# Norm, transposes and routing of a mixture's tokens by pairs of tiles inside the attention before it, and its results added and normed by pairs inside the attention after it

## Chip, cores, metric

The kernel runs on one core of one Trainium2 chip. The metric is the device time of one execution in microseconds (us); the median of five runs of the kernel before is 2369.61. The engines are PE (matrix multiply, with its weight loads shown apart as PEld), DVE (vector), ACT (scalar, activation tables), POOL (GpSimd) and SP, which only issues transfers.

## What is computed

Four layers in sequence, each an attention and a feed-forward part with a layer norm after each. x has 1024 tokens of 256 values in fp32. The change lies between the first attention, the first mixture of experts and the second attention. From the reference:

```python
# layer 0, attention: windowed, two softmaxes per head, 16 heads
    out = jnp.einsum('bhqk,bhkd->bhqd', diff, v)
    return out.transpose(0, 2, 1, 3).reshape(B, S, H * hd) @ Wo
...
# layer 0, mixture: 8 experts, each token goes to 2 of them
    router_logits = jnp.einsum('bsh,he->bse', hidden_states, Wr)
    topk_logits, selected = jax.lax.top_k(router_logits, TOP_K)
    router_probs = jax.nn.softmax(topk_logits, axis=-1)
    for e in range(NUM_EXPERTS):
        w_e = jnp.where(selected == e, router_probs, 0.0).sum(axis=-1, keepdims=True)
        g = jnp.clip(jax.nn.silu(jnp.einsum('bsh,hi->bsi', hidden_states, Wg[e])), -7.0, 7.0)
        u = jnp.einsum('bsh,hi->bsi', hidden_states, Wu[e])
        out = out + jnp.einsum('bsi,ih->bsh', g * u, Wd[e]) * w_e
...
# layer 1, attention: causal, 16 heads of 128
    q = (x @ Wq + bq).reshape(b, h, t, dh)
    k = (x @ Wk + bk).reshape(b, t, h, dh).transpose(0, 2, 3, 1)
    v = (x @ Wv + bv).reshape(b, t, h, dh).transpose(0, 2, 1, 3)
...
def _layernorm(x, axis=-1, eps=1e-05):
    return (x - m) / jnp.sqrt(v + eps)
```

After each part, x = layernorm(x + part). In layer 1 the queries are reshaped without a transpose. So the four heads of one group of queries come from 256 consecutive rows of x, while its keys and values come from all rows.

## The kernel before

x stays on the chip as `k.x`, eight tiles of 128 tokens by 256, and beside it its transpose `k.xT`, which the projections read. `transpose_two(t)` (L163) turns two tiles with four PE transposes into one bank of PSUM and copies them to `xT` on DVE (L178). `norm_half` (L191) norms four tiles: `bn_stats` and `bn_aggr` for each (L202, L203), one square root on ACT (L221) and a reciprocal on DVE (L222), then one DVE step for each tile (L206). `power` (L211) gives the same factor without ACT: one step on DVE, then a power on POOL (L215).

The stages run one after another (L1954 on): at the start of most, four calls of `transpose_two`; at the end of attn0, ffn0 and attn1, `layernorm`. Each stage takes its own buffers, laid over those of the stage before. Inside the loops marked `in_order` (L140) the instructions of PE, ACT, DVE and POOL keep the order in which the program writes them. Instructions outside such a loop, and SP's transfers, are put among them by a planner. In the trace, for instance, the statistics of tiles 0 to 3 after attn0 run at 271 us, before attn0's loop has ended.

**attn0** (L438). 32 units, four groups g of heads by eight tiles t. Unit i makes scores for its tile (L591 and L601 on PE, maximum L609 on DVE, eight exponentials L617 on ACT), then a difference of two softmaxes (L625 to L645 on DVE, ACT and POOL). Three units later `attn0_values` transposes it (L654, copied to pt on ACT at L656), multiplies by the values (L660, copied to ot on ACT at L666), projects (L672), and DVE adds the result to x (L227). So in iteration i tile t of unit i - 3 is finished, tile 0 of the last group at i = 27 and tile 7 at i = 34. The last projections of operands (`operands`, L508), which read `xT`, are through by i = 28. After i = 31 no new unit starts: three iterations only drain.

**ffn0** (L689). It stores x to DRAM as `moe_rows` in two halves (L706) and loads the weights of all experts as `gu` and `wd` with 24 transfers of 256 KB (L712, L715). The router's logits come from 16 matmuls (L739), and each tile's two experts from `max` and `max_index` (L744, L745). From L748 on the tokens are sorted by expert into 23 blocks of 128, up to `tokens` (L824). POOL then gathers each block's rows from `moe_rows` by an indirect transfer (L853, issued at L845); two matmul steps per block, and SP stores the result to `moe_results` (L894). After the loop, for each tile and each of its two experts, a gather (L916) and a DVE step that adds it, weighted, to x (L917). Then `layernorm`.

**attn1** (L931). Weights `wq` (four), `wk`, `wv`, `wo` from a pool of ten buffers. `make_queries(g, j)` (L963) projects 256 columns of `xT` and DVE adds the bias and scales (L969), writing every sixteenth element; 16 of them make group g. `make_keys` (L974) is evicted by ACT (L979), `make_values` by DVE (L988). `pieces` (L993) lists these in order. Before the first scores (L275) `ensure` runs all 16 queries of group 0 and one piece of keys; the others go between the units of the loop at L1048.

Of the kernel before, what the change touches and what calls it, by code (L numbers as in the profile page):

```python
# [25 lines left out]
I32 = mybir.dt.int32  # L26
U32 = mybir.dt.uint32
AF = mybir.ActivationFunctionType
ALU = mybir.AluOpType
AX = mybir.AxisListType  # L30

P = 128
# [10 lines left out]
class Kit:  # L43
# [147 lines left out]
    def norm_half(self, half):  # L191
        tiles = range(4 * half, 4 * half + 4)
        stats = self.tile("st", [P, 4, 2])
        for t in tiles:
            self.add_stats(t, stats)
        rstd = self.rsqrt(stats[:, :, 1], 4, LN_EPS)
        for t in tiles:
            self.norm_tile(t, stats, rstd)

# [5 lines left out]
    def norm_tile(self, t, stats, rstd):  # L205
        self.nc.vector.tensor_scalar(  # L206
            self.x[:, t, :], self.x[:, t, :], stats[:, t % 4, 0:1], rstd[:, t % 4 : t % 4 + 1],
            ALU.subtract, ALU.mult,
        )
# [8 lines left out]
    def rsqrt(self, v, n, eps, scale=1.0, tag=None):  # L218
# [3 lines left out]
        self.nc.vector.reciprocal(r, r)  # L222
        return r

    def add_rows(self, t, y):
# [212 lines left out]
def attn0(k, a):  # L438
# [92 lines left out]
    def make_values(t):  # L531
# [11 lines left out]
        even.append(vt)  # L543

    runs = [(g, half) for g in range(4) for half in range(2)]
    with k.in_order():
        for _ in operands(*runs[0]):
# [3 lines left out]
        for i in range(len(units) + 3):  # L551
# [25 lines left out]
            if i - 1 in made:  # L577
                made[i - 1] = next(made[i - 1])
            for _ in ending:
                pass  # L580

# [107 lines left out]
def ffn0(k, a):  # L689
# [8 lines left out]
    wd = k.tile("wd", [P, 8, NC, D])  # L698
    rows = k.tile("dram", [T, D], tag="moe_rows")
    results = k.tile("dram", [blocks * P, D], tag="moe_results")  # L700
    wr = k.weights([P, NC, 8], a["L0_ffn_Wr"].rearrange("(c p) e -> p c e", p=P))
    ternary_tiles = list(ffn1_weights(k, a))
    for tile_ in ternary_tiles[:2]:
        next(tile_)
    for half in range(2):
        nc.sync.dma_start(  # L706
            out=rows[half * HALF : (half + 1) * HALF, :].rearrange("(t p) d -> p t d", p=P),
            in_=k.x[:, 4 * half : 4 * half + 4, :],
        )
    for e in range(8):  # L710
# [24 lines left out]


    ps = k.bank()[:, : NT * 8].rearrange("p (t e) -> p t e", t=NT)
    for t in range(NT):
        k.project_rows(ps[:, t, :], lambda c: wr[:, c, :], t * P)  # L739
    logits, top = small([P, NT, 8]), small([P, NT, 8])  # L740
    which = small([P, NT, 8], U32)
    nc.vector.tensor_copy(logits, ps)
    for t in range(NT):
        nc.vector.max(top[:, t, :], logits[:, t, :])  # L744
        nc.vector.max_index(which[:, t, :], top[:, t, :], logits[:, t, :])  # L745
    chosen, mine = small([P, 2, NT]), k.tile("route", [P, 2, NT, 8], tag="mine", bufs=1)
# [43 lines left out]
    nc.vector.tensor_reduce(slot, mine.rearrange("p k t e -> p (k t) e"), axis=AX.X, op=ALU.add)  # L790
    slots = k.tile("route", [P, 2 * NT], I32, tag="slots", bufs=1)
    nc.vector.tensor_copy(slots, slot)
# [42 lines left out]

    prob = k.tile("route", [P, 2, NT], tag="prob", bufs=1)
    p1, p2 = prob[:, 0, :], prob[:, 1, :]
# [5 lines left out]

    def gather(out, source, index):
        nc.gpsimd.indirect_dma_start(  # L845
            out=out, out_offset=None, in_=source,
            in_offset=bass.IndirectOffsetOnAxis(ap=index, axis=0),
        )

    taken_rows, xTs, hs, hTs = {}, {}, {}, {}  # L850
    for b in range(blocks):
        taken_rows[b] = k.tile("rows", [P, D])
        gather(taken_rows[b], rows, tokens[:, b : b + 1])  # L853

# [41 lines left out]
    with k.in_order():  # L896
        turned(0)
        for b in range(blocks + 2):
# [10 lines left out]
            if 0 <= tile_ < len(ternary_tiles):  # L909
                next(ternary_tiles[tile_], None)  # L910
                if not late and tile_ + 2 < len(ternary_tiles):
                    next(ternary_tiles[tile_ + 2])
    for t in range(NT):
        for i in range(2):
            y = k.tile("rows", [P, D])
            gather(y, results, slots[:, i * NT + t : i * NT + t + 1])  # L916
            nc.vector.scalar_tensor_tensor(  # L917
                k.x[:, t, :], y, prob[:, i, t : t + 1], k.x[:, t, :], ALU.mult, ALU.add
            )

# [10 lines left out]
def attn1(k, a):  # L931
# [5 lines left out]
    nc.sync.dma_start(out=bq, in_=a["L1_attn_bq"])  # L937
    nc.sync.dma_start(out=bk, in_=a["L1_attn_bk"])
    wq, ws, queries, keys, values = [], {}, {}, {}, {}

# [22 lines left out]
    def make_queries(g, j):  # L963
        if j == 0:
# [3 lines left out]

        nc.vector.tensor_scalar(  # L969
            queries[g].rearrange("p h (t j) -> p h t j", j=16)[:, :, :, j],  # L970
            ps.rearrange("p (h t) -> p h t", h=4), bq[:, j : j + 1], scale, ALU.add, ALU.mult,
        )

# [55 lines left out]
    def attend(g, h, half, pts):  # L1029
# [12 lines left out]
        if h == 3:  # L1042
            yield from add_up(g, half)

    beside = ffn2_weights(k, a)
    with k.in_order():
        pipe = Pipe(k)
        for count, (g, h, half, s) in enumerate(units):  # L1048
# [142 lines left out]
def attn2(k, a):  # L1191
# [249 lines left out]
    def finish(ch, half, out, outs):  # L1441
# [34 lines left out]
        for s in range(4):  # L1476
            k.norm_tile(4 * half + s, stats, rstd)
            if s % 2:
                yield
# [470 lines left out]
def four_layers(ctx: ExitStack, tc: tile.TileContext, a, out):  # L1950
# [3 lines left out]
    for stage in STAGES:  # L1954
        with k.scope(**SCOPES[stage]):

            for t in {ffn1: (), ffn2: (), attn2: (0, 2)}.get(stage, range(0, NT, 2)):
                k.transpose_two(t)
            stage(k, a)
            if stage in (attn0, ffn0, attn1, attn3):  # L1960
                k.layernorm()
# [76 lines left out]
```

## Time and profile before

| | us |
|---|---|
| median of five runs (2367.59 to 2369.75) | 2369.61 |
| the profiled execution | 2364.6 |
| its span, first to last instruction | 2362.9 |
| PE busy in the span | 2168.4 (92%) |
| DVE, ACT, POOL busy | 1225.2, 893.1, 489.5 |
| last add to x in attn0 (L227), start | 291.86 |
| first gather of rows (L845), start | 314.53 |
| first gather of results (L845), start | 404.42 |
| last DVE step that adds a result (L917), start | 426.37 |
| first scores of attn1 (L275), start | 450.50 |
| granted clock of PE over the span | 0.969 |

The profile follows one execution. Its times are from the span's start. A granted clock of 1 is PE at full speed. A share of DMA is the mean busy share of the core's 16 DMA engines. The duration shown for several matmuls on one line is from the start of the first to the end of the last. The profiled execution is 5.0 us faster than the median of the runs that were timed by themselves.

### The profile page before, as it was taken

The numbers are of one execution on the slowest core, as the hardware profiler recorded it, in microseconds if no ns is written. First come the engines' busy times: TensorE is split into PE (matmuls) and PEld (weight loads), VectorE is DVE, ScalarE is ACT, GpSimd is POOL, SyncE is SP. The second block draws the span as 40 slices with busy tenths as digits, with TensorE's granted clock in tenths as the row PEclk, the third lists the DMA queues.
The fourth block names the chain that finished last, engine by engine and source line by source line (L and its number), as shares of the span: only waits on it lengthen the run. The fifth ranks groups of instructions, "written<-read, shape, count | busy, mean of one in ns | idle before, by whom it ended". The sixth has DMA issues, their size and how long they took to land.

```text
span 2362.9 us, 25437 instructions
## 1 busy us (share of the span) xinstructions
PE 2168.4 (92%) x8595; PEld 1227.1 (52%) x8595; DVE 1225.2 (52%) x2734; ACT 893.1 (38%) x2328; POOL 489.5 (21%) x630
## 2 busy tenths in 40 slices
PE   8999777799999999998988998899999997999997
PEld 4666544466656655664444443455555564444443
DVE  5677556565665646555763445544544554222223
ACT  3666524134343434344453222454544451111111
POOL 4333122222232323321110000332222220000000
PEclk9999979899999999999999999999999998999999
DMA  5100153011101101013100010000000000111000
GB/s 168 35 19 20 62 185 109 23 41 36 50 23 60 57 27 41 18 54 126 47 2 10 28 53 27 2 1 19 1 18 10 10 1 18 36 45 45 20 1 18
DMA packets 59218, 92.24 MB, mean 39 GB/s; under 512 B 8944, under 2 KB 33584, under 8 KB 59088
## 3 DMA queue, kind: packets, MB, share of 16 engines
q1 hardware_dynamic: 54176, 78.15, 10.3%
q0 software_dynamic: 4912, 12.46, 1.9%
q8 instruction: 69, 1.13, 0.2%
q14 instruction: 61, 0.50, 0.1%
HBM read 69.76 MB, written 17.17 MB: 37 GB/s over the span
## 4 chain that ended last, share of the span: by engine, by line
PE 78%; DVE 11%; ACT 6%; issue 2%; POOL 1%; DMA 1%; SPq 0%; DVEq 0%; ACTq 0%; POOLq 0%
PE bank L152 23%; PE wide L275 10%; PE wide L297 7%; PE bank L1034 5%; PE bank L262 5%; PE bank L1811 5%; PE bank L159 4%; ACT e L617 3%; PE bank L683 3%; PE bank L1019 2%; PE bank L1402 1%; PE bank L1150 1%; PE bank L869 1%; DVE st L609 1%; PE bank L672 1%
## 5 line engine op out<-in xcount | busy, mean ns | idle before, releaser
L152 PE MATMUL bank<-xT,w 128*128 128x512 f32 (+2 forms) x1520 | 660.4, 564 | 2.0 <-DVE xT L178 1.7
L152 PEld LDWEIGHTS bank<-xT,w 128*128 128x128 f32 (+1 forms) x1520 | 286.2, 193 | 279.6 <-issue 259.6
L253 POOL TENSOR_SCALAR p<-p,st 128x128 f32<-128x128 f32 (+7 forms) x256 | 191.0, 746 | 682.2 <-DVE st L252 537.7
L275 PE MATMUL wide<-k,q 128*128 128x512 f32 (+3 forms) x768 | 290.4, 487 | 3.6 <-ACT p L245 2.7
L266 ACT COPY pt<-bank 128x512 f32<-128x512 f32 (+3 forms) x384 | 170.9, 480 | 307.8 <-PE bank L262 304.6
L275 PEld LDWEIGHTS wide<-k,q 128*128 128x128 f32 x768 | 142.5, 190 | 140.5 <-issue 124.8
L240 DVE TENSOR_REDUCE st<-wide 128x1 f32<-128x128 f32 (+7 forms) x256 | 194.0, 758 | 14.7 <-POOL p L253 0.5
L297 PE MATMUL wide<-t,w 128*128 128x512 f32 (+1 forms) x392 | 187.5, 600 | 3.9 <-DVE t L1679 2.4
L262 PE MATMUL bank<-ident,p 128*128 128x128 f32 x1152 | 169.1, 274 | 18.9 <-POOL p L253 18.9
L262 PEld LDWEIGHTS bank<-ident,p 128*128 128x128 f32 x1152 | 137.9, 141 | 83.2 <-issue 38.8
L1929 DVE TENSOR_TENSOR t<-t,bank 128x512 f32<-128x512 f32 (+1 forms) x66 | 45.4, 688 | 257.4 <-PE bank L152 257.4
L1928 ACT ACTIVATE t<-bank 128x512 f32<-128x512 f32 (+1 forms) x66 | 39.4, 597 | 324.5 <-PE bank L152 319.7
L1034 PE MATMUL bank<-pt,v 128*128 128x512 f32 (+3 forms) x384 | 139.3, 487 | 0.0
L235 DVE TENSOR_TENSOR wide<-wide,causal 128x128 f32<-128x128 f32 x256 | 74.7, 292 | 122.2 <-PE wide L275 121.1
L1811 PE MATMUL bank<-pt,v 128*128 128x512 f32 x288 | 137.2, 596 | 0.0
L245 ACT ACTIVATE p<-wide,st,factor 128x128 f32<-128x128 f32 (+7 forms) x128 | 106.4, 831 | 71.3 <-DVE st L242 70.6
L297 PEld LDWEIGHTS wide<-t,w 128*128 128x128 f32 (+1 forms) x392 | 67.9, 189 | 109.4 <-issue 47.4
L159 PE MATMUL bank<-w,xT 128*128 128x512 f32 (+3 forms) x320 | 123.5, 523 | 0.0
L245 ACT ACTIVATE p<-wide,st 128x128 f32<-128x128 f32 (+7 forms) x128 | 95.0, 742 | 65.1 <-DVE st L240 64.5
L617 ACT ACTIVATE e<-wide,st 128x128 f32<-128x128 f32 x256 | 89.8, 377 | 49.9 <-DVE st L609 34.7
L1427 ACT ACTIVATE pt<-wide 128x1024 f32<-128x1024 f32 (+3 forms) x96 | 75.4, 810 | 69.1 <-PE wide L1421 67.6
L227 DVE TENSOR_TENSOR x<-bank,x 128x256 f32<-128x256 f32 x120 | 49.8, 421 | 87.3 <-PE bank L1019 34.5
(302 smaller groups left out, 3042.6 us busy)
## 6 DMA issues: line engine op xcount, KB each, us to landing
w<-in_L_ffn_gate_up_dram SPq DMA_DIRECT2D x16, 512.0 KB
w<-in_L_attn_Wq_dram SPq DMA_DIRECT2D x12, 512.0 KB
w<-in_L_attn_Wo_dram SPq DMA_DIRECT2D x12, 512.0 KB
rows<-parts SPq DMA_DIRECT2D x16, 256.0 KB
w<-in_L_ffn_down_dram SPq DMA_DIRECT2D x8, 512.0 KB
w<-in_L_attn_Wk_dram SPq DMA_DIRECT2D x7, 512.0 KB
w<-in_L_attn_Wv_dram SPq DMA_DIRECT2D x6, 512.0 KB
moe_results<-y SPq DMA_DIRECT2D x23, 128.0 KB
```

The costliest lines, as they stand in the source:

```text
L152: self.nc.tensor.matmul(out, lhsT=weight(c), rhs=self.xcols(c, lo, n), start=c == 0, stop=c == NC - 1)
L159: self.nc.tensor.matmul(out, lhsT=self.xcols(c, lo, n), rhs=weight(c), start=c == 0, stop=c == NC - 1)
L240: nc.vector.tensor_reduce(top, scores[:, :n], axis=AX.X, op=ALU.max, negate=True)
L245: nc.scalar.activation(probs[:, :n], scores[:, :n], AF.Exp, bias=top, scale=1.0 if scale is None else scale, accum_out=total,)
L253: self.nc.gpsimd.tensor_scalar(probs[:, :n], probs[:, :n], total, 1.0, ALU.mult, ALU.mult)
L262: self.nc.tensor.transpose(ps[:, i * P : (i + 1) * P], probs[:, (lo + i) * P : (lo + i + 1) * P], self.ident,)
L266: self.nc.scalar.copy(pts[lo // 4][:, :n, slot * P : (slot + 1) * P], ps[:, : n * P].rearrange("p (b q) -> p b q", b=n),)
L275: self.nc.tensor.matmul(s[:, lo : lo + m], lhsT=query, rhs=key(lo, m), start=True, stop=True)
L297: nc.tensor.matmul(acc[m][:, half * HALF : (half + 1) * HALF], lhsT=down[:, m * P : (m + 1) * P], rhs=h, start=i == 0, stop=i == count - 1,)
L617: nc.scalar.activation(e[:, r, f, b, :], sc[:, r, f, b, :], AF.Exp, bias=top[:, at : at + 1], accum_out=total[:, at : at + 1],)
L1034: nc.tensor.matmul(out[:, lo:], lhsT=values[g, b][:, h * P : (h + 1) * P], rhs=pts[b // 4][:, b % 4, lo:], start=b == 0, stop=b == 4 * hal ...
L1811: nc.tensor.matmul(out, lhsT=values[i][:, g * P : (g + 1) * P], rhs=pts[i // 4][:, i % 4, :], start=i == 0, stop=i == b,)
```

## The change

At the end of attn0 a generator `close(t)` takes tiles t and t + 1, for t = 0, 2, 4, 6, in four steps, one per iteration: statistics of tile t; statistics of tile t + 1 and the factor (`power`, but `rsqrt` for the last pair); norm of both tiles, a store of both to `moe_rows`, and `transpose_two`; routing of both with their `max` and `max_index`. The first step follows in the iteration in which tile t is finished. The router's weights `wr` are loaded at attn0's start into a buffer of their own, and ffn0 no longer norms, transposes, stores `moe_rows` or routes.

At the end of ffn0 the gathers of results, the adding and the norm are gone. In attn1 all 16 gathers are issued first, into eight buffers of the pool `ot`. Then `close(t)` adds, norms and transposes two tiles, and after each up to six pieces of the queries of group 0 are projected. The evictions of these 16 pieces move from DVE to ACT, with the bias scaled beforehand. The transposes at attn1's start go.

```diff
+    def close(t, last=False):
+        stats = k.tile("st", [P, 4, 2], tag="stats", bufs=2)
+        k.add_stats(t, stats)
+        yield
+        k.add_stats(t + 1, stats)
+        at = t % 4
+        rstd = (k.rsqrt if last else k.power)(stats[:, at : at + 2, 1], 2, LN_EPS)
+        yield
+        for i in range(2):
+            k.norm_tile(t + i, stats, rstd[:, i : i + 1])
+        nc.sync.dma_start(
+            out=k.rows[t * P : (t + 2) * P, :].rearrange("(t p) d -> p t d", p=P),
+            in_=k.x[:, t : t + 2, :],
+        )
+        k.transpose_two(t)
+        yield
+        ps = k.bank()[:, :16].rearrange("p (t e) -> p t e", t=2)
+        for i in range(2):
+            k.project_rows(ps[:, i, :], lambda c: wr[:, c, :], (t + i) * P)
+        nc.vector.tensor_copy(logits[:, t : t + 2, :], ps)
+        for i in (t, t + 1):
+            nc.vector.max(k.top[:, i, :], logits[:, i, :])
+            nc.vector.max_index(k.which[:, i, :], k.top[:, i, :], logits[:, i, :])
...
             for _ in ending:
                 pass
+            for steps in closing.values():
+                next(steps, None)
+            if i >= 3 and units[i - 3][0] == 3:
+                t = units[i - 3][1]
+                if t % 2 == 0:
+                    closing[t] = close(t, t == NT - 2)
+                    next(closing[t])
+        for steps in closing.values():
+            for _ in steps:
+                pass
...
-    for half in range(2):
-        nc.sync.dma_start(
-            out=rows[half * HALF : (half + 1) * HALF, :].rearrange("(t p) d -> p t d", p=P),
-            in_=k.x[:, 4 * half : 4 * half + 4, :],
-        )
...
-    ps = k.bank()[:, : NT * 8].rearrange("p (t e) -> p t e", t=NT)
-    for t in range(NT):
-        k.project_rows(ps[:, t, :], lambda c: wr[:, c, :], t * P)
...
-    for t in range(NT):
-        nc.vector.max(top[:, t, :], logits[:, t, :])
-        nc.vector.max_index(which[:, t, :], top[:, t, :], logits[:, t, :])
...
-    for t in range(NT):
-        for i in range(2):
-            y = k.tile("rows", [P, D])
-            gather(y, results, slots[:, i * NT + t : i * NT + t + 1])
-            nc.vector.scalar_tensor_tensor(
-                k.x[:, t, :], y, prob[:, i, t : t + 1], k.x[:, t, :], ALU.mult, ALU.add
-            )
+    k.moe = results, slots, prob
...
+    scaled_bq = k.tile("const", [P, 16], tag="scaled_bq")
+    nc.vector.tensor_scalar(scaled_bq, bq, scale, None, ALU.mult)
...
+        if g == 0:
+            nc.scalar.activation(
+                out, ps, AF.Identity, bias=scaled_bq[:, j : j + 1], scale=scale
+            )
+        else:
+            nc.vector.tensor_scalar(out, ps, bq[:, j : j + 1], scale, ALU.add, ALU.mult)
...
+    def close(t):
+        stats = k.tile("st", [P, 4, 2], tag="stats", bufs=2)
+        for j in (t, t + 1):
+            for i in range(2):
+                nc.vector.scalar_tensor_tensor(
+                    k.x[:, j, :], gathered.pop(0), prob[:, i, j : j + 1], k.x[:, j, :],
+                    ALU.mult, ALU.add,
+                )
+            k.add_stats(j, stats)
+        at = t % 4
+        rstd = k.rsqrt(stats[:, at : at + 2, 1], 2, LN_EPS)
+        for i in range(2):
+            k.norm_tile(t + i, stats, rstd[:, i : i + 1])
+        k.transpose_two(t)
...
     with k.in_order():
+        for t in range(NT):
+            two = k.tile("ot", [P, 2, D])
+            for i in range(2):
+                gathered.append(two[:, i, :])
+                k.gather(gathered[-1], results, slots[:, i * NT + t : i * NT + t + 1])
+        for t in range(0, NT, 2):
+            close(t)
+            for _ in range(6 if pieces[0][:2] == (make_queries, 0) else 0):
+                if pieces[0][:2] == (make_queries, 0):
+                    project_next()
         pipe = Pipe(k)
...
-            for t in {ffn1: (), ffn2: (), attn2: (0, 2)}.get(stage, range(0, NT, 2)):
+            mine = {ffn0: (), attn1: (), ffn1: (), ffn2: (), attn2: (0, 2)}
+            for t in mine.get(stage, range(0, NT, 2)):
                 k.transpose_two(t)
             stage(k, a)
-            if stage in (attn0, ffn0, attn1, attn3):
+            if stage in (attn1, attn3):
                 k.layernorm()
```

The tiles `slots`, `prob`, `logits`, `top` and `which` move from ffn0's buffers to ones that last. `norm_tile` takes its factor as one column, and `gather` becomes a method of the kit; neither alters what runs.

## The prediction

> **What bounds the kernel now.** I read the page first: PE is busy for 92% of the span, and the chain that ended last lies on PE for 78%. The forty slices show where that isn't so. I then took the chain of waits piece by piece between two stages, then the timeline there, and last the busy time by stretches. The change touches two such places, so its worth is read there and not from the 92%.
>
> The end of the first attention (attn0) and the start of the mixture (ffn0), from the timeline:
>
> ```profile
> 259.26 0.18 DVE L625 RECIPROCAL st<-st 128x4 f32<-128x4 f32 x1 [1.82 <-ACT e L617]
> ...
> 274.88 1.28 ACT L221 ACT_TABLE_LOAD   x1
> ...
> 289.13 0.38 SPq L712 DMA_DIRECT2D gu<-in_L_ffn_Wg_dram  x1
> ...
> 291.86 0.42 DVE L227 TENSOR_TENSOR x<-bank,x 128x256 f32<-128x256 f32 x1 [3.92 <-PE bank L672]
> ...
> 305.13 0.25 DVE L748 CAST route<-route 128x8 f32<-128x8 uint32 x2
> ...
> 314.53 1.25 POOL L845 DMA_INDIRECT rows<-moe_rows,tokens  x1 [33.77 <-DVE experts L834]
> ```
>
> Columns: start and duration in us, engine, line, what it does, and in brackets the idle time before it and what ended it. The last tile is added to x at 292.28; norm, transposes and routing go on to 305.03, and only then does the sorting of tokens (L748 on) begin. The weights gu and wd start to load at 289.13, when L660 has read the last values tile at 289.10.
>
> The end of ffn0 and the start of the second attention (attn1), from the chain of waits (start, duration, what):
>
> ```profile
> 409.41 2.73 DMA rows<-moe_results,slots
> ...
> 426.86 1.29 DVE x L206 x4
> ...
> 434.04 15.69 PE bank L152 x66
> 449.74 0.02 issue
> 449.76 0.70 ACT k L979
> 450.45 0.04 issue
> 450.50 0.49 PE wide L275 x2
> ```
>
> Gathers, adding, norm, transposes, then 16 query projections and one of keys; the first scores are at 450.50. The stretches (length; busy time and instructions of PE, weight loads, DVE, ACT, POOL; granted clock, DMA share, GB/s) show PE idle first and saturated afterwards:
>
> ```profile
> 306.00:314.00 8.00, 1.25 (x25) 1.17 (x25) 6.47 (x28) 0.71 (x1) 0.00 (x0) 0.50 1.04 341
> 412.00:427.00 15.00, 0.00 (x0) 0.00 (x0) 7.69 (x22) 0.30 (x1) 9.37 (x10) 0.50 0.33 97
> 434.00:450.00 16.00, 15.72 (x67) 12.63 (x65) 11.12 (x17) 0.24 (x1) 0.00 (x0) 0.97 0.00 1
> 450.00:975.00 525.00, 512.86 (x2009) 319.99 (x2010) 302.63 (x688) 214.08 (x483) 147.20 (x170) 1.00 0.12 39
> ```
>
> From 450.5 on, attn1 is PE work (512.86 of 525), the same before and after. So if its first scores come earlier by d, the end comes earlier by d.
>
> **Part 1, attn0's end.** Removed: the tail from 292.28 to 305.03, 12.75. In its place, for the last pair: wait for the routing matmuls of tiles 4 and 5 (8 x 0.16 behind L672, 0.9 past the add), their copy and max (0.65), one bn_stats and aggregate (0.55), sqrt to reciprocal (0.65, as at 429.98 to 430.61), two norms (0.75 with the hand-over, four take 1.38), four transposes (0.55; eight took 1.04 at 291.66), xT copy (0.75), eight routing matmuls (1.55; fourteen took 3.00 at 295.63 on a colder clock), copy and max (0.7): 7.05. That saves 5.7.
>
> What it adds ahead of the last add: three pairs normed, transposed and routed in the units before. In a full unit the loop is exps (2.9), pt copy, L660, scores L591 and L601, DVE's maximum L609, exps; DVE is idle 1.82 before L625 and 1.96 before L609, which holds a step of stats (0.55 to 0.7). A step that norms and transposes doesn't fit quite: the next L654 queues on PE behind transposes that wait for the norm. By walking the units: +0.25 after tile 2's add; after tile 3's, routing and stats make L625 1.1 late, then the ot copy and L672; 0.95 is left when the full units end. The table load at 274.88 in front of the ReLUs (1.28) is gone there, as these three pairs take the power on POOL; that is counted. In the drain, where L654, pt, L660, ot and L672 follow one another, nothing hides PE work: routing 2 and 3 costs 1.3, less 0.4 as L672 (3.62 at 278.17 on a cold clock) is then warmer; add, norm and transposes of 4 and 5, with L654 waiting, 1.85. Sum 3.7.
>
> The power itself: POOL's L215 took 1.05 for 128x4 and 2.90 for 128x16, so some 0.75 for two columns (an estimate), and it runs beside DVE's two-operand steps. What that can do is in the timeline:
>
> ```profile
> 244.50 1.27 POOL L503 TENSOR_TENSOR q<-t,t 128x512 f32<-128x512 f32 x1
> ...
> 244.53 1.26 DVE L626 TENSOR_TENSOR st<-st 128x4 f32<-128x4 f32 x1
> ```
>
> L626 takes 0.16 elsewhere. Of three powers, one (after tile 3) meets L625 to L633 where they are already late; I add 0.8, between 0 and 3 x 1.05. So the last add comes 4.5 late, and Part 1 is worth 5.7 - 4.5 = 1.2. (The Trainium skill, "SBUF — State Buffer", section Who interferes with whom, speaks against the power here: one lock is shared by GpSimd and a DVE step with two SBUF inputs, for the whole instruction. The row at 244.53 agrees; with all three powers paid in full the sum would be 1.5 worse.)
>
> **What else comes late.** L660 of the last unit comes 3.7 later, and gu, wd and attn1's two weights, 314 - 289 = 25 of full DMA, with it: they end near 318, while the first gather is issued near 313. In SP's queue the last moe_rows store waits for its norm near 299; loads behind it wait too, but expert 0's first weights are ahead. The trace has no gather amid a full load. Below: 0. Above: it waits out the load, 318 - 313 = 5. A gather is 128 KB, 0.4 at the 317 to 341 GB/s seen; shared evenly with another queue it takes twice that, so I take 1.0. Part 1 net: 0.2. (The Trainium skill, "DMA: Bandwidth & Descriptors", Queues, rings and completion order: an engine goes round between queues, a packet each. That would hold the gather a packet or so and keep the sum at 0.2; the lam load, small and behind others on one queue, took 13.46 in the chain, and by that row the sum would be -3.8. No row here shows two queues.) The router weights are one more small load, first used near 266. The new scaled bq is one DVE step (0.15); it can stall DVE at the start if bq, issued at 20.41 amid 356 GB/s, is late there: 0 to 3, taken as 0.
>
> **Part 2, attn1's start**, on the old clock up to the gathers. Gathers stay: 16 issues 1.25 apart from 404.42, each landing 2.75 to 3.2 after issue. Tile 1 is added at 411.48; stats 0.6, sqrt to reciprocal 0.65, norm 0.75, transposes and xT copy 1.55: 415.1. Queries for group 0 need tiles 0 and 1 alone (L967 reads 256 columns), so six start now, cold: 0.53 a matmul at 432.34, 2.1 a query, warm after some 3.7 (431.1 to 434.8 before), then 0.86 as now. Six end at 422.5. ACT evicts them (0.37 for such a tile, up to 0.65 as DVE's strided one takes), and the next sqrt queues on ACT behind the sixth: norm of pair 2 ends 424.4, transposes, then six queries to 429.9. Likewise pair 4, four queries to 435.5; pair 6, transposes to 437.8. Keys 1.75 and their copy 0.8: scores at 440.35 against 450.50. Gain 10.15. Here 16 x 0.86 = 13.8 of queries went beside gathers that end at 426, and about 4 came back as three waits for sqrt, norm and transposes. Bounds: 7 (evictions at 0.86 and more, gaps colder) and 13 (sqrt gone early).
>
> **Sum.** 0.2 + 10.15 = 10.3. The profiled execution took 2364.6 (span 2362.9 and 1.7 around it) and should take 2354.3; it lies 5.0 below the median of 2369.61, so the median becomes 2359.3.
>
> **Rivals.** (A) Part 1 pays in full: slack hides the added steps but for the 1.3 of routing, and gathers don't feel the load: gain 5.7 - 1.3 = 4.4 there, 14.5 in all, 2355.1. For it: DVE's two gaps per unit. Against: PE's order, L654 behind the transposes. 0.20. (B) Part 1 loses: loads held behind the last store, first gather late by 5 instead of 1, startup stall of 1: gain 10.3 - 5 = 5.3, 2364.3. For it: 1.04 DMA share to 314. Against: separate queue. 0.14. (C) Slower: PE never warms between the pieces of attn1's start. Fourteen queries left at 2.1 instead of 0.86 lose 17.4: 2376.7. It decides from 10.3, nine cold queries. For it: clock 0.50 through 412 to 434. Against: the gaps worked out are 1.5, and after gaps of 2.3 in attn0 only the next L601 was slow (1.92 for 1.05). 0.04. (D) The steps don't overlap at all, since in-order queues bring back what they hide: within 4 of before, 2367. For it: norm of tiles 0 to 3 already ran inside attn0, from 271.38. Against: queries can't but run while gathers do. 0.05.
>
> **How the numbers follow.** My forecast: 0.57, its own range 2356 to 2362. The predicted time is 2359.3. From A's 2355.1 less 2 to B's 2364.3 plus 1: 2353 to 2365.5, leaving out C, D and a little. 0.2% is 4.7, about what can be told from no change; 2364.9 divides. Faster: the forecast, A and most of B (0.09): 0.86. Same: rest of B and D: 0.10. Slower: C: 0.04.
>
> **What would show it.** Right: L748's cast within 2 of 305, first scores near 440, six, six and four queries with gaps of about 1.5 on PE, ACT's L221 right behind evictions. Wrong: DVE's add of a tile waiting for a DMA (x tracked as one piece), clock 0.50 past 420, a gather landing over 4 after issue, or DVE idle near 25 for bq.

## The result and the profile after

Measured beside each other, the changed kernel took 2367.09 us (26 executions, 2362.21 to 2375.32), the one before 2368.14 (48 executions): a ratio of 0.9997 with a 95% interval of 0.9992 to 1.0002, so no change that can be told. 2359.3 was predicted, 2353.0 to 2365.5. The profiled execution took 2370.73 (span 2369.0), 3.6 above the median. (In all that follows, one execution of the second repeat below, 7536 us at a mean granted clock of 0.309, is left out.)

Both places of the change, from the timeline of the changed kernel (columns as before; L659, L962, L233, L782, L226 are the new numbers of L609, the new scaled bias, L227, L748 and L845):

```profile
29.76 0.17 DVE L962 TENSOR_SCALAR scaled_bq<-bq 128x16 f32<-128x16 f32 x1 [3.09 <-DMA bq<-in_L_attn_bq_dram]
29.84 1.22 DVE L659 TENSOR_REDUCE st<-wide 128x8 f32<-128x1024 f32 x1
...
296.90 0.38 SPq L755 DMA_DIRECT2D gu<-in_L_ffn_Wg_dram  x1
...
299.63 0.42 DVE L233 TENSOR_TENSOR x<-bank,x 128x256 f32<-128x256 f32 x1 [3.78 <-PE bank L722]
...
307.58 0.25 DVE L782 CAST route<-which 128x8 f32<-128x8 uint32 x2
...
316.92 1.25 POOL L226 DMA_INDIRECT rows<-moe_rows,tokens  x1 [25.41 <-DMA gu<-in_L_ffn_Wu_dram]
```

From the last add of attn0 to the first gather of rows it is 17.29 us now and was 22.67: the shorter tail is there. But the last add comes 7.77 later, and the sum is 2.4 lost. In the first line the planner has put the scaled bias at the kernel's start. DVE stands still for 3.09 us before it; before the change it stood 2.01 in that place, and the first maximum (the second line) now comes 1.16 later than the 28.68 of before.

The same kernel at the start of attn1, on ACT:

```profile
414.74 1.28 ACT L220 ACT_TABLE_LOAD   x1 [10.73 <-DVE st L202]
416.03 0.29 ACT L220 ACTIVATE st<-stats,eps 128x2 f32<-128x2 f32 x1
421.15 0.70 ACT L997 ACTIVATE q<-bank,scaled_bq 128x256 f32<-128x256 f32 x1 [4.82 <-issue]
422.86 0.69 ACT L997 ACTIVATE q<-bank,scaled_bq 128x256 f32<-128x256 f32 x1 [1.01 <-PE bank L152]
424.17 0.69 ACT L997 ACTIVATE q<-bank,scaled_bq 128x256 f32<-128x256 f32 x1 [0.62 <-issue]
428.51 1.91 ACT L997 ACTIVATE q<-bank,scaled_bq 128x256 f32<-128x256 f32 x3 [3.65 <-remote]
430.21 0.27 ACT L220 ACTIVATE st<-stats,eps 128x2 f32<-128x2 f32 x1
434.15 0.69 ACT L997 ACTIVATE q<-bank,scaled_bq 128x256 f32<-128x256 f32 x1 [3.67 <-PE bank L152]
```

Read the brackets. The table load stands right before the sqrt and on the path. Three evictions follow PE, then ACT stands still for 3.65 us. The releaser is "remote", another core or an unknown queue, though the program plans a wait on PE alone there; the six queries' matmuls are through at 426.7. The trace also keeps the moments at which semaphores change, and there the signal that ACT waits for is PE's and late: the fourth query's last matmul is recorded as ending at 424.99, its signal comes at 428.48, and ACT starts at 428.51. The sqrt of the second pair is queued behind these evictions, so PE then idles for 4.55 and runs cold: its granted clock is 0.50 from 430.4 to 437.3, and the next evictions are again 1.7 apart (434.15, 435.86) and not 0.86, as at a clock of 1.00. In the chain of waits the stop is a piece of its own:

```profile
419.04 3.80 PE bank L152 x8
424.86 3.62 another core or an unknown queue
...
432.41 7.65 PE bank L152 x24
...
442.40 3.47 PE bank L152 x16
```

The same stretches as before the change (L997 moved the evictions from the DVE to the ACT column):

```profile
306.00:314.00 8.00, 0.99 (x12) 0.84 (x11) 6.49 (x35) 1.49 (x2) 0.00 (x0) 0.50 1.09 354
412.00:427.00 15.00, 8.90 (x28) 6.77 (x28) 6.23 (x17) 3.66 (x5) 11.43 (x12) 0.61 0.36 105
434.00:450.00 16.00, 12.78 (x49) 9.18 (x47) 8.26 (x23) 7.08 (x13) 0.00 (x0) 0.90 0.00 1
450.00:975.00 525.00, 512.90 (x2009) 320.05 (x2010) 302.56 (x688) 214.39 (x483) 147.65 (x170) 1.00 0.12 39
```

PE does now work 8.90 of the 15 us beside the gathers, where it did nothing. Still the first scores come at 450.72, against 450.50 before and 440.35 predicted. What was won between the first gather of results and the scores was lost again within that stretch and ahead of it.

A word on spread. One kernel's executions in one measurement differ by up to 13 us (in the first repeat below by 1.4), and go with the mean granted clock: in this measurement 0.973 gave 2362.2 and 0.968 some 2369 to 2371. A place where it shows is the third attention's start, from its L1150 (L1208 after) to its L1487 (L1545): 181.5 us in the profile before, 189.0 after, of code that the change does not touch. The granted clock (the number before the last two) tells of it:

```profile
1040.00:1060.00 20.00, 15.73 (x53) 10.70 (x52) 12.93 (x44) 4.01 (x8) 0.00 (x0) 0.62 0.01 4
1060.00:1120.00 60.00, 54.19 (x315) 27.17 (x313) 33.12 (x50) 24.28 (x34) 9.51 (x20) 0.94 0.28 91
1120.00:1165.00 45.00, 38.77 (x261) 19.36 (x260) 30.60 (x50) 17.21 (x26) 9.39 (x20) 0.85 0.33 103
```

In the profile before these three are 0.76, 1.00 and 0.96. The Trainium skill ("TensorE: Matmul & The Clock Gate", Part 1: The HAM clock gate) says that the gate looks at PE's work in windows that run free of the kernel, so that one kernel warms at different points. No run here shows the windows themselves; the repeats below are in keeping with it, with 181.0 and 189.1 us for this stretch of one and the same program. So a few us in a total prove little here, and each step below is read at its place.

### The profile page after: what moved, and what is told of

Its sections match the earlier page's. It is cut to its first block, busy times and chain, and to the rows that moved or that the text cites. A ratio compares the mean times of both kernels' runs of the same rounds, so it can differ in the third digit from the quotient of the medians.

```text
span 2369.0 us, 25450 instructions
## 1 busy us (share of the span) xinstructions
PE 2178.9 (92%) x8595; PEld 1230.2 (52%) x8595; DVE 1219.0 (51%) x2726; ACT 904.6 (38%) x2345; POOL 493.5 (21%) x633
## 3 DMA queue, kind: packets, MB, share of 16 engines
q1 hardware_dynamic: 54208, 78.15, 10.3%
## 4 chain that ended last, share of the span: by engine, by line
PE 79%; DVE 10%; ACT 6%; issue 2%; DMA 1%; POOL 1%; SPq 1%; another core or an unknown queue 0%; ACTq 0%; DVEq 0%; POOLq 0%
PE bank L152 23%; PE wide L281 10%; PE wide L303 7%; PE bank L1063 5%; PE bank L268 5%; PE bank L1869 5%; PE bank L159 4%; PE bank L733 3%; ACT e L667 2%; PE bank L1048 2%; PE bank L1460 2%; PE bank L722 1%; PE bank L1208 1%; PE bank L897 1%; PE wide L1473 1%
## 5 line engine op out<-in xcount | busy, mean ns | idle before, releaser
L159 PE MATMUL bank<-w,xT 128*128 128x512 f32 (+2 forms) x288 | 116.0, 540 | 0.5 <-ACT v L541 0.5
L233 DVE TENSOR_TENSOR x<-bank,x 128x256 f32<-128x256 f32 x120 | 49.8, 421 | 89.0 <-PE bank L1048 34.5
```

Of the source, the lines that this page charges most:

```text
L159: self.nc.tensor.matmul(out, lhsT=self.xcols(c, lo, n), rhs=weight(c), start=c == 0, stop=c == NC - 1)
```

## The experiments

Six measurements were made in all, the first being the result above; each of the five others on a chip of its own. The place to look at is the time from the first gather of results to DVE's first step on the scores: 46.60 us before the change.

**The changed kernel, unedited, four more times.**

> The changed kernel as it is, run again. Its first trace showed DVE's L659 1.16 us late at the start (behind the scaled bq, which waits for bq), a table load of 1.28 in front of the first sqrt of attn1, and ACT standing still for 3.65 in front of the fourth query eviction (424.86 to 428.51), with a releaser that the trace does not know. Theory: all three belong to the program and are there again, at the same instructions; first scores of attn1 at 450.7 within 1. Rival: the stop of 3.65 is chance of one execution; then it is missing here, and the first scores come near 444. Time: 0.9997 of before, within 0.001, by either.

> The changed kernel, nothing edited, a third time. So far it took 2362.2 to 2375.3 us (26 executions) in one measurement and 2357.2 to 2358.6 (5) in another. Theory: the change's own sequence is the quick one of the second measurement (first scores of the second attention about 440 us from the start, matmuls of the eviction stretch 420 to 445 at a granted clock of 1.00), and what differs is where the granted clock falls in places whose PE load is at the border (48 to 54, 240 to 264, 1040 to 1165 us) and one stop of ACT of 3.65 us at 424.9; then this run again shows no such stop, a median between 2356 and 2367, and executions whose time goes with the mean granted clock (0.974 near 2357, 0.968 near 2369). Rival: the stop belongs to the kernel; then ACT stands still again for 3 to 4 us between two query evictions, scores come at 449 to 451, and the median is 2365 to 2369.

> The changed kernel again, beside three of the others on one chip. So far: 2362.2 to 2375.3 us (26 executions) with a stop of ACT of 3.65 us in the profile, then 2357.2 to 2358.6 (5) and 2356.8 to 2361.1 (5) with no stop; at one and the same mean granted clock the first lies 3.8 to 4.4 us above the others (0.973: 2362.2 against 2358.4; 0.972: 2365.5 against 2361.1). Theory: without the stop the change is worth about 11 us, first scores 440 to 441, median 2357 to 2361. Rival (the stop comes with some loads of the program): it is there again, first scores 449 to 451, and the median 2363 to 2369.

> The changed kernel, as the control for the run beside it. So far two chips showed no stop (first scores 440.7 to 441.0, about 2358) and two showed one of 3.5 to 3.65 us, in which the engine that empties PE's banks stands still although only a PE signal is planned before it, and starts again 0.15 to 1.1 us after the last packet of the gathers of results (first scores 451.3, 2364.6 to 2367.1). Theory (the stop goes with the chip): one of these two pictures, whole; rival (it goes with the load of the program): something between, or both in the executions of one measurement.

| changed kernel | us, median (range; executions) | ratio to before beside it, 95% | first gather of results to scores |
|---|---|---|---|
| the result | 2367.09 (2362.21 to 2375.32; 26) | 0.9997 (0.9992 to 1.0002) | 44.58, stop |
| first repeat | 2357.65 (2357.16 to 2358.59; 5) | 0.9950 (0.9937 to 0.9963) | 38.79 |
| second | 2357.87 (2356.75 to 2361.09; 5) | 0.9955 (0.9942 to 0.9968) | 38.76 |
| third | 2364.57 (2359.72 to 2371.33; 12) | 0.9981 (0.9970 to 0.9992) | 44.64, stop |
| fourth | 2364.02 (2359.80 to 2368.78; 10) | 0.9973 (0.9962 to 0.9984) | 44.43, stop |

The kernel before took 2368.1 to 2369.6 in all five. So it is the changed kernel that has two pictures. ACT in the second repeat, at the place of the stop:

```profile
410.02 1.28 ACT L220 ACT_TABLE_LOAD   x1 [10.75 <-DVE stats L203]
...
418.14 0.69 ACT L997 ACTIVATE q<-bank,scaled_bq 128x256 f32<-128x256 f32 x1 [1.01 <-PE bank L152]
419.40 0.69 ACT L997 ACTIVATE q<-bank,scaled_bq 128x256 f32<-128x256 f32 x1 [0.58 <-PE bank L152]
```

and the chain of waits there, which has no foreign piece:

```profile
414.32 7.65 PE bank L152 x24
424.32 5.20 PE bank L152 x24
431.86 3.47 PE bank L152 x16
```

Three pieces of queries, six, six and four, the last two at 0.87 a query, and scores near 440.2: the prediction's picture. The fourth query's last matmul ends at 420.23 here, and its signal comes at 420.24. Where the stop shows, it is there in all executions, as far as times tell: at a mean granted clock of 0.973 they took 2361.8 to 2363.7 in the three measurements with a stop, and 2357.6 to 2359.7 in the two without. The interval is 5.8 longer with a stop. In the result 3.0 of this are there at the second pair's transposes; the other 2.8 come after them, as those transposes and the six queries behind them took 1.14 and 7.65 us and not 0.78 and 5.20, at the granted clock of 0.50.

**One part alone.**

> Only the first half of the change: norm, transposes, store and routing by pairs in attn0; the results are gathered, added and normed at the end of ffn0 as before, and attn1 starts as before, with no scaled bq. Theory: the tail is 5.3 shorter but the last add 5 later and the first gather 0.4 slower to land; first gather of rows at 314.3 within 1.5 (before 314.53), time within 1 of before (0.9996 to 1.0004). Rival: the tail's 12.75 is mostly gained and the whole loss lies in attn1: first gather at 309 to 311, time 4 to 5 less than before (0.998).

> The first attention and the routing as before; the additions and norms by two tiles inside the second attention as in the change, with the scaled bias at its place behind the first pair. Theory (the gain is all in Part 2, 10.15 us at the first scores by the prediction's sum, and Part 1 nets nothing): first gather of results at 404 to 405, first scores 439 to 441 against 450.5 before, and a time 8 to 11 under before's. Rival 1 (Part 1 and Part 2 both pay some): 3 to 6 under before's. Rival 2 (in-order queues bring Part 2 back): within 4 of before.

Part 1 alone (attn0's end as in the change; results added and normed as before): 2367.73 (11 executions) beside 2369.49, a ratio of 0.9990 (0.9981 to 0.9998). Its last add is 5.2 us late, the tail 5.4 shorter, the first gather of rows at 314.37 against 314.53. Part 2 alone, with the bias behind the first pair: 2357.01 (5) beside 2369.58 and beside 2357.87 for both parts; ratio 0.9943 (0.9931 to 0.9956), interval 37.77. So Part 2 holds the gain and Part 1 gives about nothing (1.8; within 1 was expected). For Part 2 the expectation was missed: the gain is 12.6 and not 8 to 11, the first gather is at 406.17 and not at 404 to 405, and the first scores at 443.41 and not at 439 to 441, which is 7.1 earlier than before. The other 5.5 lie behind the scores, in code that the change does not touch, and go with a mean granted clock of 0.970 to 0.973 beside 0.966 to 0.970.

**The scaled bias, and the table load.**

```diff
-    nc.vector.tensor_scalar(scaled_bq, bq, scale, None, ALU.mult)
...
         for t in range(0, NT, 2):
             close(t)
+            if t == 0:
+                nc.vector.tensor_scalar(scaled_bq, bq, scale, None, ALU.mult)
```

> Only the scaling of bq is moved, from the planner's choice at the kernel's start to behind the first pair in attn1. Theory: at the start L659 begins at 28.7 again instead of 29.8, the first projection of attn0 at 51.0 instead of 53.6, and all that follows is 2.6 earlier: time some 2.6 less than e1 (0.9989 of it). Rival: the wait at the start is absorbed within the first units of attn0, since ACT's exps set the pace there, and the time stays within 0.5 of e1.

It took 2361.59 (5 executions), the unedited kernel beside it 2357.65: 3.9 more, so neither the theory (2.6 less) nor its rival (within 0.5) was met. The first maximum of attn0 comes at 28.50 instead of 29.31, but the gain is gone by the first add to x (54.78 against 53.99): the granted clock from 48 to 54 us was 0.72 in this execution and 1.00 in the other. So this pair can't price the edit. All the runs with both parts can, if profiles of like clock are compared, at the issue of the first gather of results:

| granted clock at 48 to 54 us, at 240 to 264 us | bias late | bias early |
|---|---|---|
| 1.00, 1.00 | 401.1, 401.4 | 401.9, 402.3 |
| 0.72 to 0.78, 1.00 | 402.5 to 403.3 (six runs) | 403.9 |
| 0.72 to 0.78, 0.86 | 405.6 | 406.7, 406.7 |

So the early stall costs some 0.5 to 1.4 us there, while rows of different clock lie up to 4.8 apart.

The sqrt's result lay in a buffer that POOL had used last. So the sqrt had two waits, one on DVE and one on POOL. In the trace the wait on DVE is an instruction of its own, ahead of the table load, so the load comes after the statistics. In Part 2 alone, where POOL makes no powers, the load ran early without any edit (403.64, the sqrt at 413.97). With a tag of its own the sqrt has one wait in the whole change too:

```diff
-        rstd = k.rsqrt(stats[:, at : at + 2, 1], 2, LN_EPS)
+        rstd = k.rsqrt(stats[:, at : at + 2, 1], 2, LN_EPS, tag="rs")
```

> As e2, and the factor of attn1's pairs has buffers of its own, so that its sqrt waits for DVE alone and no longer for POOL as well. Theory: with two waits the one for DVE was put on the table load, which so stood on the path; with one wait the load runs early, as before the change. The first sqrt then follows the statistics within 0.1 instead of 1.4, first queries 1.3 earlier, first scores 1 to 1.5 earlier than e2. Rival: the queries then wait for the same later thing (the stop on ACT, the landing of the gathers), and the first scores don't move.

> The change with the late bias and the one-wait sqrt, as before (2353.6 then, 4.1 under the unedited change on the same chip). If the two edits are worth what their places in the trace say (table load 1.28 us off the path before the first pair, startup up to 1.2) this is 0 to 2.5 us under the unedited change beside it, and first scores come 0 to 1.5 earlier; more than that is the granted clock in the stretch from 1040 to 1165 us.

With both edits: 2353.58 (6), 4.1 under the unedited kernel beside it, ratio to before 0.9942 (0.9925 to 0.9959); on another chip 2363.49 (7), 1.1 under it, 0.9970 (0.9959 to 0.9981). The sqrt follows its statistics at once, with no table load ahead of it:

```profile
411.04 0.30 ACT L220 ACTIVATE rs<-stats,eps 128x2 f32<-128x2 f32 x1 [9.35 <-DVE stats L203]
```

The interval from the gather to the scores falls from 38.87 to 38.18, where 1 to 1.5 was expected. The first transposes do come 1.3 earlier behind the first gather (8.98 instead of 10.30), but the granted clock goes to 1.00 at 420.1 in this run as it did at 420.4 with the late bias alone, so 0.7 of the 1.28 comes through. The 4.1 of the total is not shown to come from the edits: the first scores are no earlier than the unedited kernel's (440.71 against 440.51), the executions range from 2351.3 to 2362.7, and the fast ones have a mean granted clock of 0.975 to 0.977 beside 0.973 to 0.974. On the second chip the stop was there with these edits too (2.83), so they don't remove it, and the interval is the unedited kernel's (44.60 beside 44.64).

**The evictions back on DVE.** In the kernel with both edits, `if g == 0:` in `make_queries` becomes `if g < 0:`.

> Late bias, one-wait sqrt, and the sixteen query evictions of the first group back on the vector engine. Theory: the change was right to move them, since the additions and statistics of the next pair (3.1 us on the vector engine, done by 417.3 in the change, beside the evictions on ACT) now stand behind six evictions of 0.65 us, so that PE waits some 2.3 us more before each of the three later pairs: first scores 446 to 449, time 4 to 8 above the kernel without this edit, with the evictions on the vector engine and no query eviction on ACT. Rival: the gathers' landing sets the pairs, and the engine of the evictions is worth nothing: within 1.5.

2376.6 (11 executions), 13.1 above the kernel without this edit beside it (4 to 8 was expected), and 0.26% above the kernel before (1.0016 to 1.0036). The first scores come at 461.24 (446 to 449 was expected), the interval is 59.25 beside 44.60. The next pair's additions now stand behind six evictions on DVE, so PE is kept waiting:

```profile
430.30 1.13 PE L171 MATMUL bank<-ident,x 128*128 128x128 f32 x4 [8.45 <-DVE x L206]
431.23 7.90 PE L152 MATMUL bank<-xT,w 128*128 128x256 f32 x24
444.01 1.13 PE L171 MATMUL bank<-ident,x 128*128 128x128 f32 x4 [4.88 <-DVE x L206]
```

The first wait holds the stop of this chip; the second, 4.88, was expected near 3.9 (1.6 + 2.3). What the expectation left out is that PE is cold after such a wait (granted clock 0.50 from 426.2 to 436.4 and from 443.2 to 450.0), so that the six queries behind it take 7.9 us and not 5.35. In the stop it is DVE here that stands still, for 2.89, released by "remote". So here the stop goes with the engine that empties PE's banks, and not with ACT. The change was right to move the evictions.

**The next pair closed between the queries.** In the change the second pair's statistics are ready at 417.3 (in the kernel with both edits), but its sqrt waits on ACT until 423.0, behind six evictions. So with both edits:

```diff
-        for t in range(0, NT, 2):
+        close(0)
+        k.transpose_two(0)
+        nc.vector.tensor_scalar(scaled_bq, bq, scale, None, ALU.mult)
+        for t in range(2, NT, 2):
+            fill(2)
             close(t)
...
+            fill(2)
+            k.transpose_two(t)
+            fill(2)
```

`fill(n)` projects up to n queries, and `close` no longer transposes.

> Late bias and one-wait sqrt, and the next pair closed between the queries: two queries, the additions, statistics, sqrt and norm of the next pair, two queries, its transposes, two queries. In the change the next pair's sqrt stands on ACT behind six query evictions (stats ready at 417.3, sqrt at 423.0) and PE stands still 1.6 us before each of three pairs' transposes and 0.1 to 0.6 behind them. Theory: these gaps close, 4.7 to 6.5 us; first scores near 434.5 to 436 against 440.7, and the time 4 to 7 under the kernel with late bias and one-wait sqrt (2353.6 in its measurement), so 2347 to 2350 and 19 to 22 under before's. Rival: the evictions' 0.86 each on ACT set the pace and the gathers' landing (1.25 us apart) the pairs; then 0 to 2 and 2352 to 2354.

> The next pair closed between the queries. Its first scores came 5.5 us earlier (435.25 against 440.71), yet its time was 2356.2 and the third attention's stretch, from its first folded state to its last addition, took 192 us instead of 185. Theory: that stretch varies by 8 us with the granted clock alone, whatever comes before it; then at least one execution here shows 0.975 or above and lies at 2346 to 2349. Rival: coming earlier brings it into the lower clock every time; then all executions stay at 0.972 or under and at 2353 to 2357.

> The next pair closed between the queries, a third time, as the control. Without a stop its first scores come at 435.3 (as measured once), with one at 438 to 440 (438.1 once); time 2353 to 2357 either way, since the stretch from 970 to 1165 us has varied by 8 us from one execution to the next.

PE in the kernel with both edits alone, and then in this one:

```profile
424.07 0.78 PE L171 MATMUL bank<-ident,x 128*128 128x128 f32 x4 [1.58 <-DVE x L206]
...
431.62 0.78 PE L171 MATMUL bank<-ident,x 128*128 128x128 f32 x4 [1.58 <-DVE x L206]
...
440.71 0.49 PE L281 MATMUL wide<-k,q 128*128 128x128 f32 x2 [0.78 <-ACT k L1007]
```

```profile
420.51 0.60 PE L171 MATMUL bank<-ident,x 128*128 128x128 f32 x4
...
426.15 0.78 PE L171 MATMUL bank<-ident,x 128*128 128x128 f32 x4
...
435.25 0.49 PE L281 MATMUL wide<-k,q 128*128 128x128 f32 x2 [0.78 <-ACT k L1007]
```

The brackets before the transposes are gone and the scores come 5.5 earlier: the interval is 32.77, 32.67 in another measurement, and 37.27 where the stop shows. The times: 2356.20 (5), ratio 0.9943 (0.9930 to 0.9956); 2354.25 (5), 0.9932 (0.9919 to 0.9945), 10.3 under the change beside it; 2346.24 (4), 0.9905 (0.9889 to 0.9922). In the first of these the gain did not show, as the third attention's start, the stretch measured above, took 187.6 us, and 180.7 in the kernel with both edits alone. The expectation that one execution of the next measurement would be at 0.975 or above failed (0.973 and 0.974 in all five); in the third, three of four were at 0.976 to 0.978 and took 2344.1 to 2347.3. So coming early does not bring the low clock by itself. The third time lies below what was expected for it (2353 to 2357), with the scores at 433.22. This version is faster than the kernel before in all three measurements. Beside the change it stood twice: 10.3 under it on the chip with the stop, and 1.7 under it on one without (2356.20 against 2357.87).

**The last four gathers held.** The stop began after three or four evictions and ended 0.3 to 1.1 us after the last packet of the gathers (six profiles). So the gathers of tiles 6 and 7 were put behind the third pair's additions, into buffers of tiles 4 and 5, with both edits:

```diff
-        for t in range(NT):
+        for t in range(6):
...
             close(t)
+            if t == 4:
+                fetch(6, twos[4])
+                fetch(7, twos[5])
```

> Late bias, one-wait sqrt, and the last four of the sixteen gathers of results held until the third pair is added (about 428 us), so that the first twelve end some 5 us earlier, near 419.5. Theory (where a chip shows the stop, it lasts while gathered rows move beside matmuls and ends with their last packet): on such a chip the stop at 422 to 425 is gone or ends by 420.5, and a shorter one may come beside the held four (428 to 434); first scores 441 to 445. Rival (the stop has nothing to do with the gathers' end): it stays 2.8 to 3.6 us long and ends at 425 to 429. On a chip without the stop both say the same: the last pair's rows land near 434.5 instead of 424.6, its norm waits for them, and first scores come 0 to 3 us after 440.7.

> The same with the last four gathers of results held until the third pair is added (first of them at about 423 instead of 418.6). Theory (on a chip with the stop, it comes when the last four gathers follow the first twelve without a gap): no stop here on any chip, first scores 435.5 to 438, and on a chip with the stop 1 to 3 us before the control's, on one without 0 to 2.5 behind it. Rival (holding them hid the stop by chance): the stop of 2.8 us or more is there as in the control.

First the unedited change on that chip, with the stop:

```profile
421.31 0.69 ACT L997 ACTIVATE q<-bank,scaled_bq 128x256 f32<-128x256 f32 x1 [0.60 <-issue]
424.92 0.69 ACT L997 ACTIVATE q<-bank,scaled_bq 128x256 f32<-128x256 f32 x1 [2.92 <-PE bank L152]
426.34 1.15 ACT L997 ACTIVATE q<-bank,scaled_bq 128x256 f32<-128x256 f32 x2 [0.74 <-remote]
```

then the kernel with the last four held, on the same chip:

```profile
422.13 0.69 ACT L996 ACTIVATE q<-bank,scaled_bq 128x256 f32<-128x256 f32 x1 [1.02 <-PE bank L152]
423.33 0.69 ACT L996 ACTIVATE q<-bank,scaled_bq 128x256 f32<-128x256 f32 x1 [0.51 <-PE bank L152]
424.19 0.69 ACT L996 ACTIVATE q<-bank,scaled_bq 128x256 f32<-128x256 f32 x1 [0.17 <-PE bank L152]
...
428.77 1.07 POOL L226 DMA_INDIRECT ot<-moe_results,slots  x1 [7.91 <-DVE x L1081]
```

No stop shows: interval 38.13 against 44.43, scores at 443.24 (441 to 445 expected), and 2359.65 (4 executions) against 2364.02 (10). The run beside it has neither edit, but on another chip the two edits left stop and interval as they were, so the holding is what is left; it is one profile on one chip. No stop came beside the held four either, which move from 428.8 on, at a granted clock of 1.00. So it isn't enough that gathers move beside matmuls, as the theory had it; twelve did so here, and then four. The pair of runs with the next pair closed early fell on a chip that has no stop, so it says nothing of it; there holding the gathers made the scores 1.7 later (interval 34.38 against 32.67) and the time 2357.36 (5) against 2346.24 (4), the rest of it at a lower clock.

## Why the prediction was wrong

**The step that failed** is in Part 2: "six end at 422.5 ... norm of pair 2 ends 424.4", and with it "scores at 440.35" and "gain 10.15". The sum had no wait within these six evictions but that for PE's matmuls. In the result's profile ACT stands still for 3.65 us there, for a signal of PE that comes 3.5 us after the matmul's recorded end. From the first gather of results to the scores the sum had a gain of 10.2; it was 2.0 in the result (46.60 to 44.58). Without the stop it is 7.8, as two repeats show. The scores were to come 10.35 earlier in the result's profile and came 0.22 later: 5.8 of that is the stop with the cold queries behind it, 2.4 is missing without a stop too (the table load first), and 2.4 is the first gather of results, which was to be issued 0.2 earlier and was issued 2.2 later. The row that the working lacked was not to be found: before the change PE does nothing beside these gathers (0.00 of 15 us), so nothing that empties its banks could be late there. The bounds of 7 and 13 were then set from waits between engines that the trace knew, and "below" should have reached further down for an overlap that the trace had never shown. Rival D hit the time (2367) with a false reason: the queries do run beside the gathers.

**What made 7.8 of 10.2** on the chips without a stop: the table load before the first sqrt, 1.28, not counted since "sqrt to reciprocal 0.65" was read where the load had run free. One tag takes it off the path. The rest is small: queries and evictions as predicted at 0.86 apart (an eviction takes 0.69, not 0.37 to 0.65, and is hidden), PE's gaps before the transposes 1.58 (1.5 predicted), first queries cold and then warm.

**Part 1** was right in its mechanism: the tail 5.4 shorter (5.7 predicted), the last add later by 5.2 in Part 1 alone, and by 3.2 to 7.8 in the unedited kernel (4.5), a power on POOL 0.69 to 0.73 (0.75). The first gather of rows came from 2.2 earlier to 2.4 later in the unedited kernel (1.2 earlier predicted). That scatter is larger than the term, so the runs neither confirm the 1.2 nor refute it; it goes with the granted clock at 48 to 54 and 240 to 264 us: 0.72 and 0.86 in the result and the third repeat, 1.00 and 1.00 in the first and second. Two smaller terms came out lower: the last packet of the first gather came 0.0 to 1.0 later behind its issue than before (1.0 predicted; 0.2 in the result), and the 0.8 for a power on POOL that holds DVE up did not show: beside two of the powers DVE's L676 took 0.17 us in the result, and 0.16 in most other places (0.89 beside another POOL step, L509, at 247.60).

**The scaled bias** did stall DVE (0 taken, 0.7 to 1.2 at the first maximum), and some 0.5 to 1.4 us are still there at the first gather of results.

**The sum** was met on the two chips without a stop, 2357.65 and 2357.87 against 2359.3, 11 to 12 under the kernel before; but in part by luck. In the first repeat the scores come 9.99 earlier, of which 7.8 are the interval (10.2 predicted) and 2.2 an earlier start (0.2 predicted), in a run whose granted clock was 1.00 in both of the stretches just named. And the profiled execution was 7.4 shorter than the profiled one before, not 10, so the total follows the scores only within the scatter of the clock. With the stop the change is worth from nothing to 5.5.

**Still open** is what the stop is. Shown: it appears in three of six measurements (with the change or a kernel made from it), was there in four different kernels on one chip, hits ACT or DVE, ends about with the last packets of the gathers, and was absent when the last four were held by 5 us, on one chip. What the waiting engine lacks is a signal of PE: in the result it comes 3.5 us after the matmul's recorded end, and two more follow within 0.8 (429.24, 429.30). With the next pair closed early, on the chip with the stop, ACT and DVE, which both empty banks of PE there, stood still at once:

```profile
423.21 2.61 ACT L996 ACTIVATE q<-bank,scaled_bq 128x256 f32<-128x256 f32 x4 [4.57 <-remote]
423.96 0.69 DVE L178 COPY xT<-bank 128x512 f32<-128x512 f32 x1 [5.81 <-remote]
```

Not shown: why the signal is late. One rival was not tested, the recording of the profile itself. The gathers of results signal their landing 256 times. On the three chips without a stop the traces hold 255 or 256 of these, but 113 to 132 in the six profiles with a stop, 162 in the one with the last four held on a chip that had the stop, and 87 in the profile before, where PE does nothing beside them. So the stop goes with chips on which the recording loses signals, and no run here tells whether it would be there without a recording.

## What to carry to other kernels

Work that is put under transfers where none ran before has no row that prices the overlap: keep the lower bound near no gain there, and measure on more than one chip before a verdict. When an engine serves two streams in program order, look at what the next stream's first small step is queued behind; here a sqrt behind six evictions cost PE 1.6 us three times, and interleaving won 5.5. Read such gains at their own place, since the total moves by as much with the granted clock.

## Not expected of the hardware

- On some chips, ACT or DVE stood still for some 2.8 to 5.8 us for a signal of PE that came late, with the kernel before on the same chips as quick as elsewhere (2369.5).
- With two waits on the sqrt, one of them stood as an instruction of its own ahead of the table load, and the load of 1.28 came onto the path; with one wait it ran early.
- The third attention's start took 181 to 189 us for one program, going with a granted clock of 0.85 to 1.00 at 1120 to 1165.
